# Graph layers on one core: part of the edges summed by count matrices in the last two steps, a second and shorter list of gathers, and node products in the order as written

## The chip, the core and the metric

The kernel runs on one core of a Trainium2 chip. A core has a matrix engine (TensorE, in the profile PE, its weight loads PEld), a vector engine (VectorE, DVE), an activation engine (ScalarE, ACT), a general engine (GpSimd, POOL) and 16 DMA engines. The metric is the time of one execution on the device, in microseconds. The kernel before takes 6621.72 us (median of three, 6620.99 to 6621.94).

## The reference

There are 10,000 nodes with 512 numbers each and 160,000 edges, sorted by destination. All is float32.

```python
h = relu(layernorm(x))                                   # layer 0
h_all = einsum('nd,rdf->nrf', h, rel_W) + rel_b          # four relations
agg = segment_sum(h_all[src, edge_type], dst) / max(deg, 1)
x1 = layernorm(h + h @ self_W + self_b + agg)
x = x + layernorm(x1 + gelu(x1 @ W1 + b1) @ W2 + b2)
h = relu(layernorm(x))                                   # layer 1
for W_self, W_neigh, b in ((W_self1, W_neigh1, b1), (W_self2, W_neigh2, b2)):
    agg = segment_sum(h[src], dst) / max(deg, 1)
    h = relu(h @ W_self + agg @ W_neigh + b)
return x + h
```

The loop at the end makes the last two steps of the title. Each sums 160,000 rows of 512 numbers, picked by `src`, into 10,000 destinations, and then makes two 512 x 512 products for each node.

## The kernel before

Nodes are handled in 79 blocks of 128 (the last has 16). The program has four stages.

*Stage 1, node products.* Each block is normalised, transposed and multiplied by five matrices. Beside that a generator (`step`) makes the edge lists in pieces: first the runs of equal destinations, then for each pair of blocks the rows to gather.

```python
def products(g):
    ...
    for c in range(nb):
        h = hg[:r, c, :]
        nc.scalar.activation(h, xg[:r, c, :], AF.Relu, bias=sc[c][1], scale=sc[c][0])
        hT = ap_.tile([P, KC, P], F32, name="hT")
        transposed(psT, hT[:, :, :r], h, r)
        nc.vector.tensor_tensor(h, h, bself[:r], op=OP.add)
        nc.vector.tensor_tensor(xg[:r, c, :], xg[:r, c, :], ln2b[:r], op=OP.add)
        for j, w in enumerate([wself] + wrel):
            pm = psM.tile([P, D], F32, name="pm")            # four buffers
            for k in range(KC):
                nc.tensor.matmul(pm[:r], hT[:, k, :r], w[:, k, :], ...)
            ...                                              # add of the bias on VectorE
        nc.scalar.dma_start(hall_d[n0:n0 + r, :], ...)
        if b0 + c >= 2:
            next(step, None)                                 # one piece of the lists
```

*How a block's edges are summed (stages 2, 3 and 4).* The first T = 11 edges of each of the 128 destinations are the block's own: each is one gather of 128 rows of 512 numbers that VectorE adds straight on. What a destination has beyond that is packed into OT = 5 further gathers for the block, and into two rest gathers ("tails") shared by 4 and by 16 blocks. Those rows are brought to their destinations by a product with a 0/1 matrix (`hot`). Gathered rows live in a ring of RING = 28 buffers.

```python
T = 11 * E // (16 * N)
OT = 5
OT_LAST = 3
SPANS = (4, 16)
...
def gather(b, table):
    def rows(n, idx, name="rows", bufs=RING):
        t = gat.tile([P, D], F32, name=name, bufs=bufs)
        nc.gpsimd.indirect_dma_start(out=t[:n], out_offset=None, in_=table,
                                     in_offset=bass.IndirectOffsetOnAxis(ap=idx, axis=0))
        return t[:n]
    for lv, n in enumerate(SPANS):
        if b < full and b % n == 0:
            tails[lv] = rows(P, srow[lv][:, b // n:b // n + 1], f"tail{lv}", 2)
    others = [rows(P, orow[:, b, t:t + 1]) for t in range(OT if b < full else OT_LAST)]
    if b < full:
        others += tails
    return others, [rows(P, row[:, b, t:t + 1]) for t in range(own(b))]

def sums(b, others, hot):
    ...
    for t in order:
        nc.tensor.matmul(pa[:r], hot[:, t, :r], others[t], start=..., stop=...)
    return pa

def add(b, pa, mine):
    for t in mine:
        nc.vector.tensor_tensor(pa[:r], pa[:r], t[:r], op=OP.add)
```

*Stage 2* sums layer 0's edges this way and runs its two wide products, four blocks at a time. *Stages 3 and 4* are the last two steps; both have this loop, stage 3 with `h1_d` to `h2_d`, stage 4 with `h2_d` to the output:

```python
for i, b in enumerate(blocks):
    ...
    if q and c == 0:
        load(q + 1)                                  # four blocks of h_d, one group ahead
    if i + 1 < len(blocks):
        hot = hots(blocks[i + 1])
    pa, mine = held
    add(b, pa, mine)
    m = ip.tile([P, D], F32, name="mb")
    nc.scalar.activation(m[:r], pa[:r], AF.Copy, scale=rdeg[:r, b:b + 1])
    po = psO.tile([P, D], F32, name="po3")
    hT = hTs.pop(b)
    for k in range(KC):
        nc.tensor.matmul(po[:r], hT[:, k, :r], wss[:, k, :], start=(k == 0), stop=False)
    if before:
        finish(*before)                              # the block before: wns products, bias, relu, store
    if i + 1 < len(blocks):
        turn(blocks[i + 1])
        held = begin(blocks[i + 1], hot, h_d)        # gathers and hot products of the next block
    mT = ip.tile([P, KC, P], F32, name="mTb")
    transposed(psT, mT[:, :, :r], m[:r], r)
    before = (b, po, mT)
```

Of the kernel before, what the change touches and what calls it, by code (L numbers as in the profile page):

```python
# [8 lines left out]
F32 = mybir.dt.float32  # L9
# [12 lines left out]
def kernel(  # L22
# [32 lines left out]

    nc = tc.nc
# [18 lines left out]


    T = 11 * E // (16 * N)
    OT = 5
    OT_LAST = 3
# [3 lines left out]

    ROUNDS = 12
    PAD = P

    W = 36
    TAGS = 4 + 3 * NL
    FAR = 2 * SPAN * P
    WT = 2 * W + TAGS  # L90
    assert N % P and R * N <= 1 << 16 and 2 * T + WT <= 2 * P and OT * WT <= 512
    assert (4 + 3 * NL) * NB <= 1024 and 3 * NL * NB <= 512
    assert 4 * OT * P <= R * N and OT_LAST < OT and full % 2 == 0

    def own(b):

        return T if b < full else 0

# [13 lines left out]

    ident = const.tile([P, P], F32, name="ident")
# [9 lines left out]


    row = const.tile([P, full, T], I32, name="row")
    orow = const.tile([P, NB, OT], I32, name="orow")
    srow = [const.tile([P, -(-full // n)], I32, name=f"srow{i}") for i, n in enumerate(SPANS)]
    loc = const.tile([P, NB, OT + NL], F32, name="loc")
    fits = const.tile([1, 1], I32, name="fits")
    bad = const.tile([P, 5], F32, name="bad")  # L130
# [39 lines left out]
    def runs(ep, ep2, pse, found):  # L170
# [32 lines left out]
        yield  # L203
# [30 lines left out]
        for i in range(ROUNDS):  # L234
            w = slice(8 * i, 8 * i + 8)
            nc.vector.max(out=top[:, w], in_=key)
            if i + 1 < ROUNDS:
                rest = ep2.tile([P, EC], F32, name="m")
                nc.vector.match_replace(out=rest, in_to_replace=top[:, w], in_values=key,
                                        imm_value=0.0)  # L240
                key = rest
            if i % 2:
                yield
# [29 lines left out]
        for i in range(ROUNDS):  # L273
# [14 lines left out]
            if i % 2:  # L288
                yield
# [18 lines left out]
        nc.vector.tensor_tensor(deg, first[:, 1:], first[:, :P], op=OP.subtract)  # L308

# [25 lines left out]
        bounds = ep.tile([NB, 3 * NL, P], F32, name="bounds")  # L335
        nc.vector.tensor_copy(first_over, over)
        done = 0
        for lv, n in enumerate(SPANS):
# [22 lines left out]
            for i, v in enumerate((ov, upto)):  # L361
                w = bounds[:, 3 * lv + i, :]
                nc.vector.tensor_scalar(w, bounds[:, 3 * lv - 3 + i, :] if lv else v,
                                        float(-P if lv else -OT * P), 0.0, op0=OP.add, op1=OP.max)
                nc.vector.tensor_scalar(w, w, skip, None, op0=OP.add)
            nc.vector.tensor_scalar(bounds[:, 3 * lv + 2, :], ov, shift, 64.0, op0=OP.add,
                                    op1=OP.add)
            nc.vector.tensor_scalar(bounds[:, 3 * lv + 2, :], bounds[:, 3 * lv + 2, :], 0.0, None,
                                    op0=OP.max)
            yield  # L370
        for names, vs in ((("first", "deg", "from", "upto"), (first[:, :P], deg, ov, upto)),
                          ([f"{k}{lv}" for lv in range(NL) for k in ("sfrom", "supto", "sbase")],
                           [bounds[:, i, :] for i in range(3 * NL)])):
# [6 lines left out]
        nc.vector.memset(bad[:, 3:5], 0.0)  # L380
# [3 lines left out]
        nc.vector.tensor_scalar(bad[:NB, 3:4], upto_b, float(-P), over, op0=OP.is_lt, op1=OP.add)  # L384
        nc.vector.tensor_reduce(room, deg, op=OP.max, axis=mybir.AxisListType.X)
        nc.vector.tensor_tensor(room, room, lanes_b, op=OP.subtract)
        nc.vector.tensor_scalar(bad[:NB, 4:5], room, float(W), None, op0=OP.is_gt)
        pf = pse.tile([P, 512], F32, name="pe")
        nc.tensor.matmul(pf[:1, :5], ones[:, :1], bad, start=True, stop=True)
        count = ep.tile([1, 1], F32, name="count")  # L390
        nc.vector.tensor_reduce(count, pf[:1, :5], op=OP.add, axis=mybir.AxisListType.X)
        nc.vector.tensor_scalar(fits, count, 0.0, None, op0=OP.is_equal)
# [4 lines left out]
    def lists(ep, ep2, pse, found):  # L397

        tags = ep.tile([P, NB, TAGS], F32, name="tags")
        tag_i = ep.tile([P, NB, TAGS - 2], I32, name="tag_i")  # L400
        nc.vector.memset(tags[:, :, 0:1], 1.0)
        nc.gpsimd.iota(tags[:, :, 1], pattern=[[0, NB]], base=0, channel_multiplier=1,
                       allow_small_or_imprecise_dtypes=True)
        for i, n in enumerate(SPANS):
            of = tag_i[:, :, 2 + 2 * NL + i]
            nc.gpsimd.iota(of, pattern=[[1, NB]], base=0, channel_multiplier=0)
            nc.vector.tensor_scalar(of, of, n - 1, None, op0=OP.bitwise_and)
        for i, name in enumerate(["from"] + [f"sbase{lv}" for lv in range(NL)]):
            hi, lo = tag_i[:, :, 2 * i], tag_i[:, :, 2 * i + 1]
            nc.vector.tensor_copy(lo, found[name])  # L410
            nc.vector.tensor_scalar(hi, lo, 4, None, op0=OP.logical_shift_right)
            nc.vector.tensor_scalar(lo, lo, 15, None, op0=OP.bitwise_and)
        nc.vector.tensor_copy(tags[:, :, 2:], tag_i)
        nc.vector.memset(orow[:, full:, :], 0)
        nc.vector.tensor_scalar(rdeg, found["deg"], 1.0, None, op0=OP.max)
        nc.vector.reciprocal(rdeg, rdeg)
        iota_s = ep.tile([P, OT * P], F32, name="iota_s")
        nc.gpsimd.iota(iota_s, pattern=[[1, OT * P]], base=0, channel_multiplier=0,
                       allow_small_or_imprecise_dtypes=True)
        of_span = ep.tile([P, SPAN], F32, name="of_span")  # L420
        nc.gpsimd.iota(of_span, pattern=[[P, SPAN]], base=0, channel_multiplier=0,
                       allow_small_or_imprecise_dtypes=True)
# [921 lines left out]
```

## Time and profile before

| | |
|---|---|
| time, median of three | 6621.72 us |
| profiled execution | 7289.75 us, span 7287.9 us |
| mean granted TensorE clock | 0.878 |
| busy: PE, DVE, ACT, POOL | 5630.5, 3658.1, 1016.8, 3806.5 us |
| DMA | 1361.47 MB, mean 187 GB/s |
| gathers of the last two steps | 1716 own, 786 of others, 50 tails |
| one add of a gathered row on VectorE | 699 ns |
| one gather on POOL | 960 to 973 ns |

One execution was recorded by the hardware profiler. Engines run beside each other, so the busy times overlap. "Idle before, releaser" says what ended an engine's wait; "issue" is a wait that nothing in the profile explains. The profiled execution is about a tenth longer than the timed ones; a duration in the profile is that of the profiled execution.

### The profile page before, as it was taken

The page shows a single profiled execution, that of the slowest core. Times are in us where ns is not written, and L with a number is a line of the kernel's source. Part 1 is how long each engine was busy: PE and PEld are TensorE (multiplying, and loading weights), DVE is VectorE, ACT ScalarE, POOL GpSimd, SP SyncE. Part 2 cuts the span into 40 slices and gives each one's busy share as a digit, 9 for nine tenths or more (in the row PEclk, how much of TensorE's full clock was granted, in tenths as well). Part 3 has the DMA queues.
Part 4 walks back from the last instruction along what each step waited for, and adds up shares of the span by engine and source line. Part 5 has one row for each costly group of instructions (what it writes and reads, how often), then busy time and mean ns, then how long its engine had stood idle before and what let it go on. Part 6 is the DMA issues. An engine that isn't in the chain of part 4 may idle for free.

```text
span 7287.9 us, 49954 instructions
## 1 busy us (share of the span) xinstructions
PE 5630.5 (77%) x14251; PEld 2543.5 (35%) x14251; DVE 3658.1 (50%) x7302; ACT 1016.8 (14%) x1667; POOL 3806.5 (52%) x3927
## 2 busy tenths in 40 slices
PE   8999999976899888897676666666666666666666
PEld 3444444433334333343333233333232233332232
DVE  5457777334666666665344344333333444444444
ACT  1000000002233223232211011001010000000000
POOL 0000010026666666666266666666656666666665
PEclk9999999987999999998888888888887888887888
DMA  4222222246677777776366666666666777777775
GB/s 156 101 99 99 104 94 93 93 142 191 214 222 225 227 218 225 225 228 207 125 199 207 207 207 208 207 207 204 207 205 206 218 220 218 218 217 216 221 220 171
DMA packets 456993, 1361.47 MB, mean 187 GB/s; under 512 B 71746, under 2 KB 71746, under 8 KB 446578
## 3 DMA queue, kind: packets, MB, share of 16 engines
q0 software_dynamic: 308768, 1008.91, 46.8%
q1 hardware_dynamic: 136146, 266.29, 10.3%
q10 hardware_dynamic: 11792, 82.97, 2.8%
q8 instruction: 114, 1.87, 0.1%
q14 instruction: 173, 1.42, 0.1%
HBM read 1150.89 MB, written 207.01 MB: 186 GB/s over the span
## 4 chain that ended last, share of the span: by engine, by line
PE 34%; issue 21%; another core or an unknown queue 19%; ACT 3%; DVE 3%; POOL 2%; DMA 2%; ACTq 0%; POOLq 0%; DVEq 0%; SPq 0%
PE pa L687 9%; PE ph L783 6%; PE pm L620 5%; PE po L794 5%; PE po L991 3%; PE po L1025 3%; DVE pa L699 2%; POOL rows L660 2%; PE pT L167 1%; ACT hTb L168 1%; DMA rows<-h_d,row 1%; ACT mTb L168 1%; ACT mb L1021 0%; PE pT L771 0%
## 5 line engine op out<-in xcount | busy, mean ns | idle before, releaser
L699 DVE TENSOR_TENSOR pa<-pa,rows 128x512 f32<-128x512 f32 x2574 | 1798.6, 699 | 906.1 <-issue 571.5
L660 POOL DMA_INDIRECT rows<-h_d,row x1716 | 1669.4, 973 | 906.0 <-issue 423.0
L1025 PE MATMUL po<-wss,hTb 128*128 128x512 f32 (+1 forms) x1264 | 710.5, 715 | 652.1 <-ACT hTb L168 536.3
L687 PE MATMUL pa<-rows,hot 128*128 128x512 f32 (+1 forms) x2358 | 1096.2, 611 | 55.5 <-issue 31.9
L660 POOL DMA_INDIRECT rows<-hall_d,row x858 | 855.9, 998 | 492.6 <-issue 196.3
L620 PE MATMUL pm<-wrel,hT 128*128 128x512 f32 (+1 forms) x2528 | 1101.0, 593 | 14.4 <-DVE ha L623 14.4
L991 PE MATMUL po<-wns,mTb 128*128 128x512 f32 (+1 forms) x1264 | 662.0, 673 | 439.0 <-ACT mTb L168 306.3
L660 POOL DMA_INDIRECT rows<-h_d,orow x786 | 754.6, 960 | 400.8 <-issue 218.9
L620 PEld LDWEIGHTS pm<-wrel,hT 128*128 128x128 f32 (+1 forms) x2528 | 478.0, 189 | 622.1 <-issue 595.9
L687 PEld LDWEIGHTS pa<-rows,hot 128*128 128x128 f32 (+1 forms) x2358 | 458.9, 195 | 665.2 <-issue 631.6
L783 PE MATMUL ph<-x1T,w1s 128*128 128x512 f32 (+2 forms) x1344 | 587.0, 590 | 117.9 <-ACT hid L785 88.4
L1025 PEld LDWEIGHTS po<-wss,hTb 128*128 128x128 f32 (+1 forms) x1264 | 277.8, 231 | 1024.0 <-ACT hTb L168 589.5
L660 POOL DMA_INDIRECT rows<-hall_d,orow x393 | 373.3, 950 | 450.3 <-SPq L1340 326.5
L794 PE MATMUL po<-w2s,hid 128*128 128x512 f32 (+1 forms) x1264 | 560.9, 595 | 30.5 <-issue 23.2
L991 PEld LDWEIGHTS po<-wns,mTb 128*128 128x128 f32 (+1 forms) x1264 | 266.8, 216 | 816.2 <-issue 483.0
L687 PE MATMUL pa<-tail,hot 128*128 128x512 f32 x936 | 469.0, 617 | 78.0 <-issue 72.7
L997 DVE TENSOR_TENSOR po<-po,bss 128x512 f32<-128x512 f32 (+1 forms) x79 | 55.0, 696 | 805.5 <-remote 705.9
L493 POOL DMA_INDIRECT win<-rec_d,at x79 | 74.9, 948 | 719.7 <-issue 631.4
L623 DVE TENSOR_TENSOR ha<-pm,brel 128x512 f32<-128x512 f32 (+1 forms) x316 | 217.1, 687 | 424.1 <-PE pm L620 424.0
L783 PEld LDWEIGHTS ph<-x1T,w1s 128*128 128x128 f32 x1344 | 259.8, 201 | 414.1 <-issue 311.4
L1001 DVE TENSOR_TENSOR ob<-po,bss 128x512 f32<-128x512 f32 (+1 forms) x79 | 54.5, 689 | 663.4 <-remote 293.6
L794 PEld LDWEIGHTS po<-w2s,hid 128*128 128x128 f32 (+1 forms) x1264 | 236.2, 190 | 313.4 <-issue 301.8
(238 smaller groups left out, 4165.3 us busy)
## 6 DMA issues: line engine op xcount, KB each, us to landing
hall_d<-ha ACTq DMA_DIRECT2D x78, 1024.0 KB
hb<-h_d SPq DMA_DIRECT2D x38, 1024.0 KB
rows<-h_d,row POOLq DMA_INDIRECT x1716
xs<-xs_d SPq DMA_DIRECT2D x39, 512.0 KB
xr<-xr_d SPq DMA_DIRECT2D x39, 512.0 KB
xn_d<-xr SPq DMA_DIRECT2D x39, 512.0 KB
h_d<-h SPq DMA_DIRECT2D x39, 512.0 KB
xg<-in_x_dram SPq DMA_DIRECT2D x19, 1024.0 KB
```

The lines of the kernel that those rows point to most:

```text
L167: nc.tensor.transpose(p[:, k, :r], rows[:, k * P:(k + 1) * P], ident[:r, :r])
L168: nc.scalar.copy(dest, p[:, :, :r])
L493: nc.gpsimd.indirect_dma_start(out=win[:, c, :], out_offset=None, in_=rec_d, in_offset=bass.IndirectOffsetOnAxis(ap=at[:, c:c + 1], axis=0))
L620: nc.tensor.matmul(pm[:r], hT[:, k, :r], w[:, k, :], start=(k == 0), stop=(k == KC - 1))
L623: nc.vector.tensor_tensor(ha[:r, j - 1, :], pm[:r], brel[:r, (j - 1) * D:j * D], op=OP.add)
L660: nc.gpsimd.indirect_dma_start(out=t[:n], out_offset=None, in_=table, in_offset=bass.IndirectOffsetOnAxis(ap=idx, axis=0))
L687: nc.tensor.matmul(pa[:r], hot[:, t, :r], others[t], start=(t == order[0]), stop=(t == order[-1]))
L699: nc.vector.tensor_tensor(pa[:r], pa[:r], t[:r], op=OP.add)
L783: nc.tensor.matmul(ph[:, :n], w1s[:, k, f * P:(f + 1) * P], self.xT[:, k, :n], start=(k == 0), stop=(k == KC - 1))
L794: nc.tensor.matmul(po[:r], self.hid[:, f, c * r:(c + 1) * r], w2s[:, f, :], start=(f == 0), stop=(f == FC - 1))
L991: nc.tensor.matmul(po[:r], mT[:, k, :r], wns[:, k, :], start=False, stop=(k == KC - 1))
L1025: nc.tensor.matmul(po[:r], hT[:, k, :r], wss[:, k, :], start=(k == 0), stop=False)
```

## The change

The change has four parts.

1. In stage 1, for each destination up to six distinct sources below 1536 are found, and a one is scattered for each into a matrix of counts in device memory: for every block a matrix of sources by 128 destinations, in bfloat16. The remaining edges ("high") are written out as a compact list.
2. In the last two steps, the rows of those 1536 sources are held on chip (12 tiles of 128 rows) and not gathered. Their part of a block's sum is 12 count matrices times rows. The product is made in float32r; for accuracy each row is split in two parts, its float32r rounding and the rest, so there are 24 products.
3. The high edges get a list of their own, with 10 own gathers and 4 others instead of 11 and 5 (with the tails 14.3 a block). It is made during stage 3 from the compact list, a block's part in each turn of the loop and 16 blocks ahead of its use; the first 16 blocks of stage 3 and the last block of 16 nodes in both steps use the first list. Stage 2 keeps the first list. The ring has 24 buffers instead of 28, and nodes are loaded by two blocks instead of four.
4. Stage 1 runs in the order as it is written (`manual_schedule`), with the next block's statistics, normalisation and transposition placed between a block's products, two additions moved to GpSimd, and the list maker cut into smaller pieces, six a block.

```diff
-    T = 11 * E // (16 * N)
-    OT = 5
+    LB = 12
+    LOW = LB * P
+    SHIFT = (LOW - 1).bit_length()
+    CAP = 6
+    HIGHS = 40
+    ls1 = Lists(11 * E // (16 * N), 5, 36)
+    ls2 = Lists(10 * E // (16 * N), 4, HIGHS - 10 * E // (16 * N))
+    count_d = [dram.tile([CELLS + 8 * P, 1], BF16, name=f"count_d{b}") for b in range(full)]
...
-        RING = 28
+        RING = 24
```

Stage 1, the search for low sources and the scatter of their counts, for each pair of blocks:

```diff
+        def part(b0, halves):
...
+            for c in range(2):
+                nc.vector.max(out=top[:, c, :], in_=live[:, c, :])
...
+            for j in range(CAP):
+                for c in range(2):
+                    st = nc.gpsimd.indirect_dma_start(
+                        out=count_d[b0 + c], in_=ones_b, in_offset=None,
+                        out_offset=bass.IndirectOffsetOnAxis(ap=at[:, c, j:j + 1], axis=0))
+            yield
+            for c in range(2):
+                now, take = key[:, c, :], top[:, c, :]
+                for i in range(HIGHS // 8):
+                    rest = ep2.tile([P, ALL], F32, name="rest")
+                    nc.vector.match_replace(out=rest, in_to_replace=take, in_values=now,
+                                            imm_value=0.0)
+                    now, take = rest, high[:, c, 8 * i:8 * i + 8]
+                    nc.vector.max(out=take, in_=now)
+                yield
...
         def look_up(b0, nb, win):
+            if b0 < full:
+                yield from part(b0, halves)
```

(An edge that repeats a source of the same destination stays among the high edges, so each count is a one or a zero.)

Stage 1, the order of the products:

```diff
     with ExitStack() as s:
+        s.enter_context(tc.manual_schedule())
...
+        for i, (g, c) in enumerate(seq):
...
+            ahead = {0: stats, 1: normed, 3: turned} if i + 1 < len(seq) else {}
+            for j, w in enumerate([wself] + wrel):
+                pm = psM.tile([P, D], F32, name="pm")
+                for k in range(KC):
+                    nc.tensor.matmul(pm[:r], hT[:, k, :r], w[:, k, :], ...)
+                if j in ahead:
+                    ahead[j](*seq[i + 1])
...
+                    nc.gpsimd.tensor_tensor(h, h, bself[:r], op=OP.add)
+                if i >= 3:
+                    next(step, None)
```

The last two steps:

```diff
+        def begin(ls, b, hot, table, counts=()):
+            others, mine = gather(ls, b, table)
             pa = psA.tile([P, D], F32, name="pa")
+            for k, (count, parts) in enumerate(counts):
+                for i in range(2):
+                    nc.tensor.matmul(pa, count, parts[:, i, :], start=(k + i == 0), stop=False)
...
+                def load_counts(b):
+                    if b < full and list_of(b) is ls2:
+                        raws[b] = ip.tile([P, LOW], BF16, name="raw")
+                        nc.sync.dma_start(raws[b], count_d[b][:CELLS, :]...)
+                def counts(b):
...
+                    for k in range(0, LB, LB // 2):
+                        t = ip.tile([P, LB // 2, P], F32R, name="count")
+                        nc.scalar.copy(t.rearrange("p k d -> p (k d)"),
+                                       raw[:, k * P:(k + LB // 2) * P])
+                        got += [(t[:, i, :], lows[:, k + i, :, :]) for i in range(LB // 2)]
+                    return got
...
+                lows = lp.tile([P, LB, 2, D], F32R, name="lows")
+                for k in range(LB):
+                    t = gat.tile([P, D], F32, name="rows", bufs=RING)
+                    nc.sync.dma_start(t, h_d[k * P:(k + 1) * P, :])
+                    nc.scalar.copy(lows[:, k, 0, :], t)
+                    nc.vector.tensor_tensor(lows[:, k, 1, :], t, lows[:, k, 0, :].bitcast(F32),
+                                            op=OP.subtract)
...
                     if i + 1 < len(blocks):
-                        hot = hots(blocks[i + 1])
+                        hot = hots(list_of(blocks[i + 1]), blocks[i + 1])
+                        counted = counts(blocks[i + 1])
+                    if i + 2 < len(blocks):
+                        load_counts(blocks[i + 2])
...
+                    next(making, None)               # stage 3 only: a piece of the second list
                     if i + 1 < len(blocks):
                         turn(blocks[i + 1])
-                        held = begin(blocks[i + 1], hot, h_d)
+                        held = begin(list_of(blocks[i + 1]), blocks[i + 1], hot, h_d, counted)
```

## The prediction

> **What bounds the kernel now.** I read first the page's busy tenths in 40 slices, to cut the program into its stages.
>
> ```profile
> PE   8999999976899888897676666666666666666666
> DVE  5457777334666666665344344333333444444444
> POOL 0000010026666666666266666666656666666665
> DMA  4222222246677777776366666666666777777775
> ```
>
> POOL shows four stretches: nothing until slice 8 (node products and edge lists), then gathers in three blocks, with a dip at slice 19. The first starts of the tiles' instructions put the borders at about 1582, 3590 and 5435 us. The table by stage for those borders (span, then busy us and instructions of PE, PEld, DVE, ACT, POOL, then granted clock, DMA share, GB/s):
>
> ```profile
> 0.00:1582.00 1582.00, 1482.81 (x4241) 685.69 (x4241) 913.43 (x3128) 111.59 (x182) 79.23 (x99) 0.97 0.28 102
> 1582.00:3590.00 2008.00, 1705.18 (x4022) 757.18 (x4022) 1235.01 (x2065) 584.50 (x932) 1255.94 (x1277) 0.91 0.69 211
> 3590.00:5435.00 1845.00, 1233.60 (x2994) 554.26 (x2994) 728.70 (x1016) 181.85 (x316) 1228.73 (x1276) 0.82 0.69 205
> 5435.00:7288.00 1853.00, 1208.87 (x2994) 546.36 (x2994) 780.99 (x1093) 138.82 (x237) 1242.55 (x1276) 0.82 0.70 215
> ```
>
> The last two rows are the two steps that the change is about: half of the span, 1276 gathers in each, PE busy two thirds. What holds them is seen in the timeline of a quiet stretch, first POOL, then PE:
>
> ```profile
> 3948.73 0.95 POOL L660 DMA_INDIRECT rows<-h_d,row  x1 [0.30 <-issue]
> 3949.99 0.95 POOL L660 DMA_INDIRECT rows<-h_d,row  x1 [0.31 <-issue]
> 3951.24 0.95 POOL L660 DMA_INDIRECT rows<-h_d,row  x1 [0.30 <-DVE pa L699]
> ```
>
> ```profile
> 3938.79 3.60 PE L991 MATMUL po<-wns,mTb 128*128 128x512 f32 x8
> 3942.22 0.60 PE L167 MATMUL pT<-ident,hb 128*128 128x128 f32 x4
> 3942.66 1.88 PE L687 MATMUL pa<-tail,hot 128*128 128x512 f32 x4
> 3944.38 4.45 PE L687 MATMUL pa<-rows,hot 128*128 128x512 f32 x10
> 3948.67 0.60 PE L167 MATMUL pT<-ident,mb 128*128 128x128 f32 x4
> 3949.10 3.60 PE L1025 MATMUL po<-wss,hTb 128*128 128x512 f32 x8
> 3952.54 3.60 PE L991 MATMUL po<-wns,mTb 128*128 128x512 f32 x8
> ```
>
> POOL issues a gather every 1.25 us (0.95 and a fixed 0.30), whatever it waits for. A block has 11 + 5 + 0.31 = 16.31 gathers, so 20.4 us of POOL. PE, when nothing holds it, is through a block in 3952.54 - 3938.79 = 13.75 us. POOL is the bound: 1276 x 1.2525 = 1598 us in a step. The profile's 1845 has about 35 us of restart (POOL's longest wait there is 33.9) and some 210 us of stalls, of which the next view names the kind:
>
> ```profile
> DVE ob L1001 <- remote: 293.6, 15, 24.9
> POOL rows L660 <- remote: 133.4, 49, 5.6
> ```
>
> DVE and ACT stand still together for up to 25 us, and POOL stops when the ring of 28 rows is full. The profiled execution took 7290 us, the timed ones 6622. I take it that most of these stalls belong to the profiled execution; with 1598 + 35 = 1633 us for each step, 6622 leaves 3356 us for the first two stages, which the profile has at 3590. That fits, so 1633 is what I predict from.
>
> **What the Trainium skill says.** *GPSIMD Engine Reference*, section 4, says that a pair of GpSimd cores writes the descriptors of a DMA issued there. The trace agrees that the cost sits on POOL: 0.95 us for a gather, the same from either table, so fewer gathers are the way to shorten a POOL-bound step. *FP8 and Floating Point Precision*, section TensorE Precision Notes: a true FP32 product makes four passes through the array, reduced-precision FP32 is truncated to FP22. In the trace each f32 product is two instructions of 0.43 us, so 0.859 us or four times 0.215. No float32r product is in the trace; one pass, 0.215 us, is my estimate from both. *TensorE: Matmul & The Clock Gate*, Part 1: the clock is gated down after idle windows. The trace agrees: 0.97 in the dense first stage, 0.82 in the two steps. A denser PE should get a better clock.
>
> **The change, part by part.** *Gathers.* Edges whose source is below 1536 leave the lists (up to six distinct ones for a node), so 11 + 5 becomes 10 + 4: 14.31 for a block. The last step has 3 + 78 x 14 + 25 = 1120 gathers, 1403 us, 195 less. The step before it uses the old list for its first 16 blocks: 3 + 16 x 16 + 62 x 14 + 25 = 1152, 1443 us, 155 less. Were POOL still the bound, that would be 350 us.
>
> *PE in a block.* One hot product less: 6 x 0.859 = 5.15 us. The 12 count matrices times two parts: 24 x 0.215 = 5.16. Own and neighbour weights as before, 8 x 0.859 = 6.87; eight transposes 0.88. Sum 18.1 us, against POOL's 14.31 x 1.2525 = 17.9. So PE goes from 13.75 to 18.1 and takes the bound over at once: of POOL's 2.5 us saved, 2.3 can be had. Where two engines are level, each other's stalls add up. The second stage shows the price: PE there needs about 20.7 us a block (14 instructions of hot products, 16 each up and down, 4 transposes), POOL 20.4, and in the timed runs the stage must be near 1780 us (3356 less some 1576 for the first). Its last gather starts at 3462, 128 us before its end; less 140 us for that drain and the beginning, 1640 over 78 blocks are 21.0 a block, 1.5% over. With PE and POOL this close I take twice that, 3%: 18.65 us.
>
> *Other engines in the steps.* DVE has 10 adds at 0.73 (the timeline has 11 in 8.03 us), a hot comparison near 0.95, the ends 0.6 to 1.3: 9 to 10 us. In the first of the steps the second list comes on top: from the first stage's rows some 25 small operations, 5 to 6 us a block. Together 15, beside 18.65. ACT gets two copies of 128 x 768, some 1.7 us, for a sum near 4. DMA loses 2 x 0.262 MB a block and gains 0.39 MB of counts: 4.7 MB in 18.65 us is 250 GB/s, what a quiet stretch (6020 to 6060 us, 248 GB/s) has at a share of 0.79. None of these is the bound.
>
> *Begin of each step.* Twelve loads of 0.26 MB, a copy and a subtraction each, through half of the ring: 15 to 25 us that hide only in part. I take 20.
>
> So the last step: 78 x 18.65 + 35 + 20 = 1510, against 1633: 123 less. The step before: 17 x 20.4 + 62 x 18.8 + 55 = 1568: 65 less.
>
> *Node products.* PE needs 79 x (20 x 0.859 + 0.44) = 1392 us and has 1582 with the lists' small products. The new work is DVE's: for a pair of blocks some 16 operations on 128 x 96 or less, 10 searches and 10 replacements over 48 numbers, about 6.5 us, so 39 x 6.5 = 255 us; the additions of bself and ln2b go to POOL and give 104 us back. DVE: 913 + 255 - 104 + 30 for the second bounds = near 1095 of 1500, 73%, cut into six short pieces a block, so that PE's four PSUM buffers bridge them. By my count 439 pieces fall into 456 places: the list ends some three blocks before the products. POOL gets 468 scatters at 1.25 (585 us) and 158 additions, for which section 3.1 of *GPSIMD Engine Reference* has about twice VectorE's time, so 1.4 us as an estimate: some 800 us of 1500. No run here shows it yet. The order as written may also close part of PE's 190 us over its minimum. I take 30 us less.
>
> *Gathers of the second stage.* Unchanged but for a ring of 24 instead of 28: 10 us more.
>
> Sum: 6622 - 123 - 65 - 30 + 10 = 6414. For what I can't see (refills, a hb load now one block ahead and not three) I add 30: 6440 us.
>
> **The rivals.** First, POOL stays the bound and PE hides: the steps lose 350, less 40 at the starts; with the first stage 6280 us. For it: PE's clock should rise; against it: 18.1 is already above 17.9. Second, the float32r product costs more than one pass, or its weight loads (0.19 us for f32 ones, hidden behind 0.43) do not hide behind 0.215. At 0.3 us the block is 20.1, level with today, and all is lost but the first stage: 6620. At two passes it would be 23 us, and the program some 400 us slower; I give that little weight. Third, the first stage grows: if the pieces on DVE or the scatters hold PE back by 2 us a block, +160 us eats nearly all: 6600. For it: in the two list stretches DVE was already busy three quarters with half of that work; against it: the work is now spread over the whole stage instead of its middle.
>
> **Range and chances.** The first rival bounds the gain, the second and third bring it to nothing. I put 8 in 10 between 6260 and 6640. Faster by 2% means under 6489; 6440 lies only 49 us below it, on a spread of some 140. Faster 0.60, within 2% 0.29, slower 0.11.
>
> **What would show it.** PE as the bound in the last step: PE busy share near 95%, granted clock above 0.9, POOL's waits ended by PE. A count product of 0.215 us from start to start; 0.3 or more is the second rival. The first stage at or under 1582 us in the profile; more is the third. 1120 and 1152 gathers. I would be wrong if the last step still ran at POOL's pace, or above 20 us a block, or if a load (raw, hb, lows) ends PE's waits.

## The result and the profile after

The changed kernel takes 6931.21 us (median of four, 6921.73 to 6938.63), the kernel before 6621.35 us (6615.35 to 6621.94) beside it. The ratio is 1.047 (95% interval 1.045 to 1.049): slower, by 310 us. The page's busy tenths of the changed kernel in 40 slices, for the three engines and the DMA engines that mattered before:

```profile
PE   8787677686777999999999679999999799999999
...
POOL 1244444443427777777774677766667577777776
...
DMA  3287697797748888888885678777777688888887
```

The last 28 slices are what was wanted: PE at nine tenths beside a POOL at seven. The first 12 are not: PE at six to eight, where it had been at nine, and DMA engines as busy as in the gathers. The first starts of the tiles' instructions put the borders at 2083, 3870 and 5455 us; the table by stage (span, then busy us and instructions of PE, PEld, DVE, ACT, POOL, then granted clock, DMA share, GB/s):

```profile
0.00:2083.00 2083.00, 1570.93 (x4254) 727.41 (x4254) 1380.90 (x5021) 130.13 (x260) 758.38 (x776) 0.87 0.69 99
2083.00:3870.00 1787.00, 1645.18 (x4026) 728.70 (x4026) 1235.40 (x2080) 590.16 (x945) 1289.78 (x1302) 0.96 0.78 242
3870.00:5455.00 1585.00, 1455.46 (x4822) 813.37 (x4822) 1137.62 (x3053) 275.01 (x439) 1099.73 (x1132) 0.95 0.75 231
5455.00:6937.00 1482.00, 1446.91 (x4710) 830.03 (x4710) 727.06 (x1029) 259.20 (x405) 1111.77 (x1117) 0.99 0.82 263
```

The last three rows were predicted at 1790, 1568 and 1510 us and are 1787, 1585 and 1482. The first was predicted at 1546 and is 2083: the whole miss, 537 us, lies in the node products and lists. Its DMA share of 0.69 goes with only 99 GB/s; the first stage before moved 102 GB/s at 0.28. So the DMA engines are not moving more, they are taking longer. The page's list of DMA issues (issue, engine, count, KB each, median us to landing) shows it at plain stores:

```profile
hall_d<-ha SPq DMA_DIRECT2D x78, 1024.0 KB, 16.2
...
count_d<-zero SPq DMA_DIRECT2D x78, 512.0 KB, 27.6
```

Three lines of the list of waits within 0 to 2083 us name what holds VectorE, PE and POOL (who waits <- for what: us in total, times, longest):

```profile
DVE ha L831 <- DMA hall_d<-ha: 232.0, 15, 27.8
PE pe L573 <- DVE kept L561: 188.7, 40, 31.1
POOL count_d L676 <- DMA count_d<-ones_b,cells: 146.4, 62, 7.5
```

A stretch of VectorE's timeline has the first two in one place (start, us, what; in brackets the idle time before it and what ended it):

```profile
1312.83 4.37 DVE L513 TENSOR_TENSOR hi<-hi,lo 128x5 f32<-128x5 f32 x1
...
1317.32 0.18 DVE L561 COPY kept<-win 128x82 bf16<-128x82 bf16 x1
1344.32 0.69 DVE L831 TENSOR_TENSOR ha<-pm,brel 128x512 f32<-128x512 f32 x1 [26.82 <-DMA hall_d<-ha]
```

VectorE stands for 26.8 us until a store of `ha`, which has two buffers, has landed. PE, whose result buffers (PSUM) VectorE empties, is busy 0.23 us of the 27 from 1317 to 1344. Just before, an operation on five numbers takes 4.37 us, while three additions run on POOL; PE waits for the copy behind it:

```profile
1313.47 1.27 POOL L798 TENSOR_TENSOR xg<-xg,ln2b 128x512 f32<-128x512 f32 x1
1314.69 1.27 POOL L835 TENSOR_TENSOR hg<-hg,bself 128x512 f32<-128x512 f32 x1
1315.91 1.26 POOL L798 TENSOR_TENSOR xg<-xg,ln2b 128x512 f32<-128x512 f32 x1
```

### The profile page after: what moved, and what is told of

Same layout as the page of the kernel before. It is cut to its first block, busy times and chain, and to the rows that moved or that the text cites. A ratio compares the mean times of both kernels' runs of the same rounds, so it can differ in the third digit from the quotient of the medians.

```text
span 6936.9 us, 62294 instructions
## 1 busy us (share of the span) xinstructions
PE 6118.5 (88%) x17812; PEld 3099.5 (45%) x17812; DVE 4481.0 (65%) x11181; ACT 1254.5 (18%) x2049; POOL 4259.7 (61%) x4324
## 5 line engine op out<-in xcount | busy, mean ns | idle before, releaser
L905 DVE TENSOR_TENSOR pa<-pa,rows 128x512 f32<-128x512 f32 x2434 | 1700.7, 699 | 1364.6 <-issue 620.8
L866 POOL DMA_INDIRECT rows<-h_d,row x1576 | 1558.0, 989 | 596.5 <-issue 185.9
L897 PE MATMUL pa<-rows,hot 128*128 128x512 f32 (+1 forms) x2078 | 980.5, 612 | 125.9 <-DVE hot L882 62.1
L894 PE MATMUL pa<-lows,count 128*128 128x512 f32 x3360 | 827.7, 403 | 0.0
L866 POOL DMA_INDIRECT rows<-h_d,orow x646 | 629.3, 974 | 234.5 <-issue 63.1
L894 PEld LDWEIGHTS pa<-lows,count 128*128 128x128 f32 x3360 | 641.0, 194 | 131.8
L676 POOL DMA_INDIRECT count_d<-ones_b,cells x468 | 459.7, 982 | 381.1 <-DMA count_d<-ones_b,cells 146.4
L1000 PE MATMUL po<-w2s,hid 128*128 128x512 f32 (+1 forms) x1264 | 558.0, 595 | 18.4 <-DVE rest L1056 18.4
L1309 PE MATMUL po<-wss,hTb 128*128 128x512 f32 (+1 forms) x1264 | 570.2, 594 | 0.0
L1237 PE MATMUL po<-wns,mTb 128*128 128x512 f32 (+1 forms) x1264 | 568.4, 592 | 1.5 <-ACT mTb L200 1.5
L826 PE MATMUL pm<-wself,hT 128*128 128x512 f32 (+1 forms) x632 | 319.0, 652 | 63.4 <-DVE at L623 48.4
## 6 DMA issues: line engine op xcount, KB each, us to landing
hall_d<-ha SPq DMA_DIRECT2D x78, 1024.0 KB, 16.2
count_d<-zero SPq DMA_DIRECT2D x78, 512.0 KB, 27.6
```

The source lines that it names most:

```text
L676: st = nc.gpsimd.indirect_dma_start(out=count_d[b0 + c], in_=ones_b, in_offset=None, out_offset=bass.IndirectOffsetOnAxis(ap=at[:, c, j:j ...
L826: nc.tensor.matmul(pm[:r], hT[:, k, :r], w[:, k, :], start=(k == 0), stop=(k == KC - 1))
L894: nc.tensor.matmul(pa, count, parts[:, i, :], start=(k + i == 0), stop=False)
L897: nc.tensor.matmul(pa[:r], hot[:, t, :r], others[t], start=(t == order[0] and not counts), stop=(t == order[-1]))
L1000: nc.tensor.matmul(po[:r], self.hid[:, f, c * r:(c + 1) * r], w2s[:, f, :], start=(f == 0), stop=(f == FC - 1))
L1237: nc.tensor.matmul(po[:r], mT[:, k, :r], wns[:, k, :], start=False, stop=(k == KC - 1))
```

## The experiments

**Theories.** A: the two-byte writes of the scatters hold the DMA engines. B: VectorE has too much to do. C: the order as written, in two halves: C1, the additions on GpSimd hold VectorE's operations; C2, the lists' small products stand in PE's program order behind VectorE's results. D: the zero fills of the count matrices (78 x 512 KB) are the load. In the first expectations C has no halves yet and takes in that the store of `ha` moved from ScalarE's queue to SyncE's.

All runs but the last two were on chips on which every kernel takes about a tenth longer (the kernel before 7289 to 7325 us), so each is compared with the kernel before on its own chip. The measure for the first stage is the start of the first own gather of layer 0's rows on POOL (the "first gather" below; gathers of others start 13 to 15 us earlier), read from one profile of each run. What follows it takes 5447 to 5512 us in all the runs there that have the new last steps, and 5679 and 5687 in the two that don't (e6_order, e0_before). So most of what sets the runs apart lies in the first stage, and a ratio also holds the rest's 65 us. Four kernels that differ only in where the spare writes go, or whether they are made (e8_skip and the three runs after it in the table), lie within 19 us; smaller differences say nothing.

| run | what it is | first gather, us | ratio to before, 95% |
|---|---|---|---|
| e0_before | kernel before | 1601 | |
| e6_order | part 4 of the change alone | 1795 | 1.026 (1.024 to 1.029) |
| e1_noscat | changed, no scatters | 1809 | 0.998 (0.996 to 1.000) |
| e8_skip | changed, spare writes skipped | 1895 | 1.014 (1.011 to 1.016) |
| e13_spread | changed, spare cells 4 KB apart | 1879 | 1.012 (1.008 to 1.016) |
| e18_64B | the same, 64 bytes apart | 1898 | 1.007 (1.005 to 1.009) |
| e19_256B | the same, 256 bytes apart | 1897 | 1.006 (1.003 to 1.008) |
| e9_after | changed kernel | 2109 | 1.035 (1.030 to 1.041) |
| e5_addsdve | changed, additions on VectorE | 2075 | 1.033 (1.029 to 1.037) |
| e10_sched | changed, scheduler's order | 2420 | 1.073 (1.069 to 1.077) |
| e14_schedskip | scheduler's order, writes skipped | 1714 | 0.986 (0.982 to 0.990) |
| e11_fix | the same, four sources a node | 1605 | 0.966 (0.964 to 0.969) |
| e15_lowfill | the same, a quarter less zeroed | 1617 | 0.972 (0.966 to 0.977) |
| e12_written | order as written, skipped, four sources | 1864 | 1.010 (1.006 to 1.014) |
| e17_adds | the same, additions on VectorE | 1813 | 0.995 (0.993 to 0.996) |
| e16_later | e12 with shared products later | 1752 | 0.984 (0.979 to 0.988) |
| e20_both | e12 with both | 1687 | 0.973 (0.971 to 0.975) |
| e21_best | e16 in the scheduler's order | 1609 | 0.962 (0.960 to 0.963) |

**The kernel before, once more.**

> The kernel before once more, for a profile of an execution near its timed 6621 us. If the long profiled execution (7290 us) was stalls of that one execution, the four stages should now be near 1576, 1780, 1633 and 1633 us, as the prediction took them. If the stages are long by nature and the timed runs short for another reason, the profile is again near 7290 us.

It took 7289.88 us with a span of 7288.1 us, and 15 executions of the kernel before on the same chip took 7272.52 to 7315.65 us. So the long time is the chip's and not the profiling's, to which the prediction had put the stalls. The waits for `remote` that it showed go with such a chip: for the changed kernel, POOL has 147.6 us of them in e9_after and none in the profile of the result.

**The order alone.** There is no second list, no scatter, no count and no zero fill; the first stage is as written, with the additions on GpSimd and smaller pieces.

```diff
-            if b0 < full:
-                yield from part(b0, halves)
...
                 def list_of(b):
-                    return ls1 if b == full or step == 0 and b < SPAN else ls2
+                    return ls1
```

> Part 4 of the change alone: the first stage in the order as written with its additions on GpSimd and the store on the SP queue, but no search for low sources, no scatters, no fills, no second list; the last two steps gather by the first list. Theories A, B and D: the first stage is 1450 to 1560 us, the total near 6600 (the last two steps as before). Theory C: the first stage stays above 1800 us, the total above 6850.

First gather at 1795 us, 194 later than before, with no edge counted at all. Part 4, which was to help, costs by itself. The store of `ha` on SyncE's queue, which this run also has, is not the cause: e11_fix below has it too and is at 1605 us.

**No scatters.** The loop of scatters does nothing, so the count matrices stay zero and the low edges are left out of the last two steps; `part`'s VectorE work and the zero fills stay.

```diff
-            for j in range(CAP):
+            for j in range(0):
```

> The changed kernel without the 468 scatters of counts (the count matrices stay zero, so the low edges are left out of the sums of the last two steps). Theory A, the scatters' 59904 writes of 2 bytes fill the DMA engines, so that the store of the node products lands late and VectorE and then PE wait for its buffer: the first stage falls from 2083 to near 1600 us, the total to near 6450. Theory B, VectorE's added list work holds PE: it is all still there, the first stage stays above 1950 and the total above 6800. Theory C, the new order and the store's move to the SP queue hold it: as B. Theory D, the 41 MB of zero fills: as B.

1809 us: 14 more than the order alone, which is within the spread, although VectorE is busy 1339.32 us up to there and not 986.22. B and D together are worth no more than that. Neither expected figure came, near 1600 or above 1950, as the order and the scatters both have a part: the remaining 300 us of 2109 belong to the scatters.

**Writes to spare cells skipped.** A node with fewer than six low sources has its other scatters sent to spare cells behind the matrix. Sources are drawn evenly, so some 0.1536 x 160,000 = 24,600 edges have a low source, while 468 scatters of 128 write 59,904 cells: some 35,300 writes are spare.

```diff
                         out_offset=bass.IndirectOffsetOnAxis(ap=at[:, c, j:j + 1], axis=0),
+                        bounds_check=CELLS - 1, oob_is_err=False)
```

> The changed kernel with a bound on the scatters' indices, so that the lanes without a low source are skipped and not written to a spare cell: 24.3 thousand writes (2.43 of 6 for a node) and not 59.9 thousand, with the same 468 instructions. Theory A, if the cost goes with the writes: about 0.59 of the 480 us are won, the first stage near 1800, the total near 6650. If the cost goes with the instructions, or by B, C or D: 6931 within 1%.

1895 us, with as many scatter instructions and as many packets of the software queue (17,504 in the first stage). That is less gain than A expected, and yet 214 us less than the changed kernel on such a chip:

> The changed kernel itself, unaltered, so that the single-part runs have it beside them. On the chip that ran the kernel before in 7296 us: theory A (two-byte writes and their descriptors fill the DMA engines): first stage about 2100 us, 220 us more than with the writes to spare cells left out (1880), and the whole about 7600 us. Theory C (the order as written, with the lists' products and the additions on GpSimd, is the whole cost): first stage no longer than about 1850 us and the whole about 7350 us, since the part without any edge counting already ended its first stage at 1780 us. If the chip is a faster one, the whole is near 6930 us, and the same differences are read against the kernel before.

The changed kernel had 2109 us there. So the 300 us are 86 for the scatters and their real writes, 214 for the spare ones.

**Why the spare writes cost so much.** Two things set them apart: their number, and that the 128 cells of one scatter lie side by side, 2 bytes apart. This run keeps the number and moves only the addresses.

```diff
-    count_d = [dram.tile([CELLS + 8 * P, 1], BF16, name=f"count_d{b}") for b in range(full)]
+    count_d = [dram.tile([2 * CELLS, 1], BF16, name=f"count_d{b}") for b in range(full)]
...
-        nc.gpsimd.iota(uncounted, pattern=[[P, 8]], base=CELLS, channel_multiplier=1)
+        nc.gpsimd.iota(uncounted, pattern=[[P, 8]], base=CELLS, channel_multiplier=1 << SHIFT)
```

> The changed kernel with one thing altered: the spare cells of a node block lie 4 KB apart, as a block's real cells of different sources do, instead of side by side (2 bytes apart). As many instructions and as many two-byte writes as in the changed kernel. Theory A1 (many two-byte writes to the same few hundred bytes wait for each other and hold the DMA engines): first stage about 1880 us, like the run that skips those writes, ratio about 1.014. Theory A2 (the number of two-byte writes fills the DMA engines, wherever they go): first stage 2080 us or more, ratio 1.035 or more.

1879 us, like the run that skips the writes. The DMA queues from 400 to 1200 us (packets, MB, share of the 16 engines), the queue of plain loads and stores (q1) and that of the gathers and scatters (q0), first in the changed kernel, then in this run:

```profile
q1 hardware_dynamic: 26188, 75.74, 71.9%
q0 software_dynamic: 8128, 2.56, 4.5%
```

```profile
q1 hardware_dynamic: 32186, 92.14, 31.0%
q0 software_dynamic: 9738, 2.97, 1.9%
```

A plain packet took 0.719 x 16 x 800 / 26188 = 0.35 us in the changed kernel and 0.310 x 16 x 800 / 32186 = 0.12 us with the spare cells apart. It isn't the scatters' own packets that fill the engines, at 4.5%: the other transfers get slower. What held VectorE goes with it: its waits for the store of `ha`, 190.3 us in e9_after from 0 to 2000 us, are gone in this run. How near is too near:

```diff
-        nc.gpsimd.iota(uncounted, pattern=[[P, 8]], base=CELLS, channel_multiplier=1)
+        nc.gpsimd.iota(uncounted, pattern=[[32 * P, 8]], base=CELLS, channel_multiplier=32)
```

> The changed kernel with the spare cells 64 bytes apart instead of 2 bytes. If only writes inside the same 64 bytes wait for each other: like the run with 4 KB, first stage about 1880 us, ratio 1.012. If nearness of a few KB is enough: like the changed kernel, 2110 us, ratio 1.035.

With 128 in place of 32:

> The changed kernel with the spare cells 256 bytes apart instead of 2 bytes. If the same line of 512 bytes is what counts, two nodes share one: first stage between 1880 and 2000 us, ratio 1.012 to 1.02. If 64 bytes count: 1880 us, ratio 1.012. If the same region of memory counts: 2110 us, ratio 1.035.

1898 and 1897 us. At 64 bytes the cost is gone, so it is not the region of memory. *DMA: Bandwidth & Descriptors* of the Trainium skill, section Specifications, says that transfers below 512 bytes are a read-modify-write. No run here shows that step. That two such writes to the same few bytes wait for each other fits A1 and is argued, not shown; the 64 bytes are this case's own figure, and nothing between 2 and 64 was tried.

**The additions, first try.**

```diff
-            nc.gpsimd.tensor_tensor(xgs[g][:r, c, :], xgs[g][:r, c, :], ln2b[:r], op=OP.add)
+            nc.vector.tensor_tensor(xgs[g][:r, c, :], xgs[g][:r, c, :], ln2b[:r], op=OP.add)
...
-                    nc.gpsimd.tensor_tensor(h, h, bself[:r], op=OP.add)
+                    nc.vector.tensor_tensor(h, h, bself[:r], op=OP.add)
```

> The changed kernel with its two additions per node block of the first stage back on VectorE, where they were before. Theory C1 (the additions on GpSimd hold VectorE's operations, and TensorE waits for those): first stage 60 to 120 us shorter than the changed kernel's. Theory B (VectorE is short of time): first stage longer by 79 x 2 x 0.45 = 70 us. Theory A (DMA): no change within 20 us.

2075 us, 34 less, which none of the three expected; the ratio is the same within its interval. VectorE took 158 additions back, and its busy time up to the first gather went from 1370.66 to 1348.55 us. So this run does not try B, which e1_noscat has answered; and C1 is not decided: the DMA engines still hold the stage.

**The scheduler's order, with and without the writes.** The kernel before lets the scheduler order the first stage; here the changed one does too.

```diff
     with ExitStack() as s:
-        s.enter_context(tc.manual_schedule())
```

> The changed kernel with the first stage's instructions ordered by the scheduler, as the kernel before has it, instead of as written; all work is kept. Theory C2 (TensorE stands behind the lists' small products in program order): first stage 150 to 250 us shorter than the changed kernel's, about 1880 us. Theory A (DMA filled by scatters and fills): at most 50 us shorter, since the same writes still have to land before the same reads.

2420 us, longer by 310: neither expectation, and against C as a whole, it seemed. The same order with the spare writes skipped:

> The changed kernel with writes to spare cells skipped and the scheduler's order in the first stage, six counted sources a node: it differs from the run of the scheduler's order alone (first stage 2370 us, ratio 1.073) by the skipped writes only, and from the best run (about 1600 us, 0.966) by 156 more scatter instructions. Theory A (the writes are the cause): first stage 1600 to 1700 us, ratio 0.965 to 0.98. Rival (the scatter instructions on GpSimd are): first stage above 1850 us.

1714 us, a little more than expected of A, and far from its rival. Under this order the same writes cost 706 us. Two of the longest waits of e10_sched (0 to 2370 us) fall to 25.4 and 30.0 us in e14_schedskip (0 to 1700 us):

```profile
DVE key L637 <- DMA win<-rec_d,at: 649.4, 31, 63.6
POOL cells L671 <- DMA count_d<-ones_b,cells: 601.8, 27, 37.9
```

POOL waits for earlier scatters to land before it can refill their index tile, and VectorE waits for edge windows that POOL issues. Why this order suffers more than the written one from the same writes was not settled further. Now fewer scatters as well, at most four sources a node, 312 instructions instead of 468 (the edges left over go to the second list, whose gathers are as many):

```diff
-    CAP = 6
+    CAP = 4
```

> The three suspects taken away together: first stage ordered by the scheduler, writes to spare cells skipped, and four sources a node counted at most instead of six (so 312 scatters instead of 468). If A and C together are the cause: first stage about 1620 to 1700 us and the whole 2 to 4% under the kernel before. If something else in the first stage holds it (the lists' VectorE work itself): first stage above 1780 us and the whole near the kernel before.

1605 us, where the kernel before starts at 1601, and 3.4% under it in all. D was tried once more on this one, with the zeros only where they are read:

```diff
-                                  zero.bitcast(BF16))
+                                  zero.bitcast(BF16)[:, :LOW])
```

> The best run so far (scheduler's order, spare writes skipped, four sources a node) with the count matrices zeroed only in the 1536 columns that are read, a quarter fewer bytes. Theory D (the zero fills still cost in the first stage): 20 to 60 us shorter than that run, ratio 0.96. Otherwise: the same within 10 us, ratio 0.966, as TensorE is busy 98% of the time there from 400 us on.

(The destination is cut alike.) 1617 us: no gain, so D falls here too.

**What is wrong with the order as written.** The same two repairs in the order as written:

> The changed kernel with writes to spare cells skipped and four counted sources a node instead of six, its first stage in the order as written. Beside the run with the same two and the scheduler's order (whole 7070 us, first stage about 1600 us, ratio 0.966): theory C2 (the order as written costs some 180 us of its own, as in the run of the order alone, 1780 against 1582): first stage 1780 to 1850 us, ratio to the kernel before 0.99 to 1.01. Rival (the order was slow only because of the writes): first stage about 1620 us, ratio 0.97.

1864 us, a little above C2's range and 259 more than the scheduler's order with the same work. What PE waits for from 200 to 1600 us:

```profile
PE pe L573 <- DVE kept L561: 77.3, 34, 3.5
PE pe L552 <- DVE of L476: 54.5, 22, 5.2
PE pe L573 <- DVE both L503: 37.0, 17, 3.9
```

L573 are small products (128 x 82) that need a copy, `kept`, which VectorE reaches only behind the dozen operations of the look-up before it. PE takes its instructions in the order as written, so the block's large products wait too: in the changed kernel it stood 5.55 us before such a product at 1317.55 us. The next run makes that copy before the look-up and the shared products one piece later:

```diff
             for t in range(nt):
                 nc.tensor.matmul(pm[:, t, :], of[:, t * P:(t + 1) * P], window, ...)
+            if b < full:
+                ...
+                nc.vector.tensor_copy(self.kept[:, j, :], window)
             got, rows, none = self.picked(pm[:, :nt], self.slot[:, :nt], 0, 2)
...
-            nc.vector.tensor_copy(self.kept[:, j, :], window)
...
                 look.finish(b0 + c, of[c], halves[:, c, :])
                 yield
+                look.shares()
```

> The changed kernel with spare writes skipped and four counted sources a node (the run in the order as written: first stage 1864 us, ratio 1.010), and in it the lists' shared products moved one piece later, with the copy that they read ahead of the ten VectorE operations it stood behind. Theory C2 (TensorE waits behind VectorE for these products, 77 + 37 us of waits from 200 to 1600 us): first stage 80 to 130 us shorter, 1740 to 1790 us, ratio 0.99 to 1.00. Theory C1 (additions on GpSimd): no change within 20 us.

1752 us, 112 less. The same waits (the lines have moved to L579 and L557):

```profile
PE pe L552 <- DVE of L476: 86.8, 36, 5.3
...
PE pe L579 <- DVE kept L557: 10.9, 10, 1.9
PE pe L579 <- DVE both L503: 3.9, 6, 1.3
```

114.3 us became 14.8; 32 went to the next such product, so 67 of the 112 us are seen in these waits. C2 holds. (The ratio, 0.984, came out below the range expected.) And the additions again, now that the DMA engines are free (the diff of e5_addsdve on e12_written):

> The same kernel with the order as written, skipped writes and four sources, and the two additions of each node block on VectorE instead of GpSimd. Theory C1 (the additions on GpSimd hold VectorE's operations): first stage 40 to 120 us shorter than 1864 us, ratio 0.995 to 1.005. Theory C2: the same or up to 50 us longer, as VectorE gets 79 x 2 x 0.45 = 70 us more to do and TensorE waits behind it, ratio 1.01 to 1.018.

1813 us, 51 less, so C1 holds too. Two lines of VectorE's groups from 200 to 1600 us (count, busy us, mean ns, idle before), first with the additions on GpSimd, then on VectorE:

```profile
L474 DVE TENSOR_SCALAR after<-iota_s,f_from 128x640 bf16<-128x640 f32 x69 | 66.0, 957 | 0.0
L495 DVE SCALAR_TENSOR_TENSOR nth<-got,slot 128x5 f32<-128x5 f32 (+1 forms) x89 | 26.3, 296 | 3.1
```

```profile
L474 DVE TENSOR_SCALAR after<-iota_s,f_from 128x640 bf16<-128x640 f32 x72 | 39.3, 546 | 0.0
L495 DVE SCALAR_TENSOR_TENSOR nth<-got,slot 128x5 f32<-128x5 f32 (+1 forms) x93 | 15.3, 165 | 3.2
```

An operation on five numbers a lane (L495) takes 165 ns and sometimes waits out a whole addition of 1.27 us. *SBUF — State Buffer* of the Trainium skill, section "SBUF: two separate sides", has a reason: a GpSimd operation and a VectorE operation that has two inputs in SBUF or runs in a two-port mode take a shared pair of ports in turns, each for its whole instruction. The trace agrees in that the additions with an input in PSUM (`ha<-pm,brel`) take 685 ns in both runs. In which mode L474 runs no trace shows. Summed over all groups of VectorE that both runs have, the work of e12_written took some 120 us longer than in e17_adds, by my estimate from these lists; the 126 additions that VectorE took back there cost 86.6 us. Both repairs together:

> Order as written, spare writes skipped, four sources, shared products later and the additions on VectorE. If the two costs are separate: first stage 1752 - 50 = about 1700 us, ratio 0.970 to 0.977. If both stood for the same VectorE backlog: first stage about 1750 us, ratio 0.983.

1687 us where 1864 - 112 - 51 = 1701 was to be expected: the two costs are separate. (This run and the next were on a faster chip; in the profile of the result, from such a chip, the changed kernel has 2088 us and not 2109.) What is left over the scheduler's order, some 80 us, was not taken apart; the longest wait of PE in its list from 200 to 1600 us is for `of`, 45.0 us.

**A version that beats both.** Spare writes skipped, four sources, shared products later, scheduler's order:

> The same without the additions moved, under the scheduler's order: the best run (0.966, first stage 1605 us) with shared products later. TensorE has 43 us of waits for those products left from 200 to 1600 us there: first stage 1570 to 1605 us, ratio 0.96 to 0.967.

6380.52 us (6375.76 to 6385.60) against 6636.41 us for the kernel before: ratio 0.962 (0.960 to 0.963). The first gather starts at 1609 us, just outside what was expected, so the later products add nothing to e11_fix that can be seen; the ratios of the two come from different chips, on which the changed kernel's own differ more (1.035 and 1.047). PE is busy 768 of the 800 us from 400 to 1200. The stores that took 16.2 and 27.6 us in the changed kernel land in (same list of the page; 4.0 and 5.6 in e20_both, with the order as written):

```profile
hall_d<-ha SPq DMA_DIRECT2D x78, 1024.0 KB, 4.0
...
count_d<-zero SPq DMA_DIRECT2D x78, 512.0 KB, 6.2
```

## Why the prediction was wrong

**The starting point: wrong in its reason.** "Most of these stalls belong to the profiled execution" is answered by e0_before: they belong to the chip. No profile of the kernel before on a faster chip is on record, so the 1633 us a step were never measured, nor the 123 and 65 us of gain; what is measured are the stages after.

**POOL bounds the two steps, PE takes over: right.** PE's timeline in the last step of the changed kernel:

```profile
6005.14 0.60 PE L199 MATMUL pT<-ident,hb 128*128 128x128 f32 x4
6005.49 5.72 PE L894 MATMUL pa<-lows,count 128*128 128x512 f32 x24
6011.05 1.88 PE L897 MATMUL pa<-tail,hot 128*128 128x512 f32 x4
...
6023.51 0.60 PE L199 MATMUL pT<-ident,hb 128*128 128x128 f32 x4
```

A block takes 6023.51 - 6005.14 = 18.4 us (18.1 worked out, 18.65 with the 3% for two level engines). PE is busy 1447 of 1482 us, at a clock of 0.99. The gathers are the 1120 and 1152 that were counted. The third sign, PE ending POOL's waits, is weak: POOL's idle time there is for the most part its 0.3 us between issues. The first rival, with POOL as the bound, did not come.

**The float32r product: nearly right.** 24 of them from 6005.49 to 6011.05 are 0.232 us each, for an estimate of 0.215. The second rival falls: the weight loads, 188 ns each, hide.

**Second stage and starts: right in size**, 1787 for 1790; the 30 us for the unseen were not needed in the last step (28 under) and about half used in the one before (17 over).

**Node products, 30 us less: wrong**, and here the whole miss lies. The third rival had the right place and a third of the size (160 us). By the runs on the chips that take longer, one profile each, there are four terms, from 1601 to 2109 us, 508 together:

- the order as written, which was to close part of PE's 190 us of idle time, opened it: 194 us more. The step that failed is "six short pieces a block, so that PE's four PSUM buffers bridge them". VectorE's load was not the point (66% in the end, 1381 us busy and not 1095). What counts is that a piece's own small product waits in PE's program order for VectorE's queue; undoing that was worth 112 us in e16_later. And "the additions of bself and ln2b go to POOL and give 104 us back" gave nothing back: moving them to VectorE again made the stage 51 us shorter in e17_adds. Some 80 us of the order stay open.
- `part`'s work on VectorE and the zero fills: 14 us, within the spread. The busy time was estimated at 255 us, with 30 for the second bounds, and is 353 (1339.32 - 986.22); that it would hardly cost anything was right.
- the scatters and their real writes: 86 us. They were counted as POOL's time only, 468 x 1.25.
- the spare writes, side by side: 214 us. "468 scatters at 1.25 (585 us)" had no term for what a scatter does to the DMA engines after it is issued. This was the largest part. The third rival named the scatters, but as something that holds PE back directly; by way of the DMA engines it was in no rival.

The gain of the last two steps was there all the time: with the first stage repaired the kernel takes 6381 us, for 6636 of the kernel before on that chip.

## What to carry to other kernels

A scatter's price is not its issue: look at what the DMA share does at constant GB/s, and give writes that nobody reads addresses far apart (64 bytes were enough here), or skip them. In an order written by hand, a small product that needs a fresh result of a busy engine stops every product behind it; put a piece of other work between the result and its use. Work moved to an engine that shares a port with the busy one can still hold it: the 158 additions on GpSimd cost 51 us here.

## What the runs showed of the hardware that was not expected

- 128 two-byte writes of one indirect scatter, 2 bytes apart, slow the other DMA traffic: a plain packet took 0.35 us in e9_after, and 0.12 in e13_spread with the same number of writes 4 KB apart. At 64 bytes apart the first stage is as short (1898 us, 1879 at 4 KB, 2109 at 2 bytes).
- A scatter that skips writes by a bounds test still costs POOL 0.99 us (mean in e11_fix), and the software queue moves as many packets (17,504 in the first stage of e9_after and of e8_skip); the first stage is 214 us shorter all the same.
- An addition of 128 x 512 on GpSimd takes 1.27 us and can hold VectorE's small operations as long (1.27 us at most in e12_written for one of 0.17); three in a row held one for 4.37 us.
